# Masked attention with a residual on one core: the first weight through another queue, the first projection between two gathers, and two pieces of work in other slots

## The chip, the core and the metric

The kernel runs on one core of a Trainium2 chip. The core has a matrix engine (TensorE; PE in the profile, with its weight loads as PEld), three engines for other arithmetic (VectorE or DVE, ScalarE or ACT, GpSimd or POOL) and a queue processor that issues transfers (SyncE or SP). Each engine works its own instructions off in order and waits for others through semaphores. Transfers that SP issues go through the queue that the profile calls q1, those of GpSimd through q0; both run on the same 16 DMA engines.

The metric is the time of one execution on the device, in microseconds. The kernel before takes 684.34 us, the median of three runs.

## What is computed

There are 8 batches of x (512 features, 1024 tokens), a mask of zeros and ones over the tokens, and two 512 x 512 weights. Queries, keys and values are the same projection; there are 8 heads of 64 features.

```python
def _L0_cond_ref(x, mask, Wq, Wo):
    xt = jnp.transpose(x, (0, 2, 1))
    q = xt @ Wq.T
    qh = q.reshape(B, T, NH, dk).transpose(0, 2, 1, 3)
    scores = scale * jnp.einsum('bhqd,bhkd->bhqk', qh, qh)
    logits = (scores * cmask + (1.0 - cmask) * NEG) * rmask
    attn = jax.nn.softmax(logits, axis=-1)
    ctx = jnp.einsum('bhqk,bhkd->bhqd', attn, qh)
    ctx = ctx.transpose(0, 2, 1, 3).reshape(B, T, D)
    out = ctx @ Wo.T
    return jnp.transpose(out, (0, 2, 1))
x = x + _L0_cond_ref(x, cond_2048, L0_cond_Wq, L0_cond_Wo)
```

A masked token gets the same scores everywhere, so its context is the mean of all values; only the kept tokens, about half, need real attention.

## The kernel before

**The data.** For each batch the kernel gathers the kept tokens, at most 543 of 1024, pads them to 544, and adds one column for the mean. To gather, it needs tokens as rows: x is loaded in two halves of four transfers (`load_half`, L384), VectorE transposes it in quarters of 32 x 32 blocks (`turn`, L395), and SP stores the rows to a buffer in DRAM (xd, L402). A search over ranks (`search`) finds the kept tokens' places. GpSimd then gathers them in five chunks, four of 128 rows and one of 32 (`gather`, L476), into tiles xin. TensorE transposes each chunk, and a copy puts it in place (`collect`, L494 and L497). `put_mean` adds the mean column from the sums of the features (`add_features`, L417).

**A pair** is two heads of a batch, 128 features; there are 32 pairs. For each the kernel projects the kept tokens in two halves (`project`, L524, tile pq), transposes the result into values (`turn_values`, L550 and L552: four chunks, then the fifth), squares them on ScalarE (`square`, L559), and on VectorE sums the squares to lengths and takes the largest (`top_of`, L565 and L572). One transpose on TensorE spreads that top (`bias_of`, L579); from it comes the bias that keeps the exponentials small. Then scores (L617, L630), exponentials (L650) and the product with the values (`weigh`, L672) follow in five chunks. `end_values` copies the contexts out; `contexts` (L766 to L777, VectorE) divides them by the sums, which travel through DRAM to be spread (`invert`). `output` (L797) multiplies a chunk of 128 tokens by the second weight, and GpSimd stores it to DRAM (od, L809). From there `fetch` (L867) gathers blocks of whole batches again, VectorE transposes them and GpSimd adds x (`finish_block`, L877 and L879), and SP stores the result (L886).

**The order** is written out by hand. `early` prepares the mask, the ranks, the first batch's rows and the first weight (`load_weights`, L935; `turn_weights`, L945 and L948). `late` gathers and projects the first pair and then runs over all pairs with five slots each: a slot (b, pr, c) holds the scores of chunk c of pair pr of batch b. `plan` puts every other task in a slot with a rank. Within a slot the tasks of rank under 5 run first, then those from 5 to 8, then the rest; `contexts` of the pair before runs in slot 3, ahead of the middle ranks where both pair and batch number are above 0, and behind them otherwise. In `plan`, `finds`, `turns`, `feats`, `takes`, `mean` and `turned` are the slots of the next batch's work, and for batches 0 to 6 `slots` and `ends` those of the fetches and the finishing of blocks. `hold` makes GpSimd wait for an exponential before a gather, so that it isn't issued too early. `warm` are matmuls whose results nobody uses.

PSUM banks come in three tags of two buffers each; a tile that takes a bank waits until the tile two before it has been read.

Of the kernel before, what the change touches and what calls it, by code (L numbers as in the profile page):

```python
# [306 lines left out]
def attention_of_kept_tokens(ctx, tc, x, mask, wq, wo, out, ident, wqT, woT, verdict, flag):  # L307


    nc = tc.nc  # L310
    B, D, T = x.shape
    P = 128
# [3 lines left out]
    NT = T // P  # L316
# [10 lines left out]
    NC = -(-LONG // P)  # L327
# [622 lines left out]
    def early():  # L950
# [38 lines left out]
        count(key, [[P, NC]], 1)  # L989
        for ri in ris:  # L990
            nc.gpsimd.memset(ri, 1.0)

        nc.vector.tensor_scalar(at, at, fold, None, ALU.add)
        for h in range(2):
# [53 lines left out]
        )  # L1048
        for i in range(NQ):
            turn(0, i, True)  # L1050
        weights["wq"] = load_weights(wq, "wq")
        for i in range(NC):
            search(0, i, True)
        for d in range(ND):
# [55 lines left out]
    def plan():  # L1110
# [26 lines left out]
        for n in range(1, B):  # L1137
            b = n - 2
            if n == 1:
                finds = [(0, 0, 0), (0, 0, 1), (0, 0, 1), (0, 1, 2), (0, 1, 4)]  # L1140
                turns = [(0, 0, 2), (0, 0, 4), (0, 1, 0), (0, 1, 1)]
                feats = [(0, 1, 2), (0, 1, 4), (0, 2, 0), (0, 2, 1)]
                takes = [(0, 1, 3), (0, 1, 3), (0, 1, 4), (0, 2, 0), (0, 2, 1)]
                mean = (0, 2, 4)
                turned = [(0, 2, 2), (0, 2, 2), (0, 2, 4), (0, 2, 4), (0, 2, 4)]
            else:
                put(b, 1, 3, load_ranks, n)
                put(b, 2, 0, load_half, n, 0)
                put(b, 3, 0, load_half, n, 1)
                finds = [(b, 3, 1), (b, 3, 2), (b, 3, 4), (b + 1, 0, 1), (b + 1, 0, 4)]  # L1150
                turns = [(b, 2, 4), (b, 3, 0), (b + 1, 0, 0), (b + 1, 0, 1)]
                feats = [(0, 2), (1, 0), (1, 1), (2, 1)]
                feats = [(b + 1, *at) for at in feats]
                takes = [(0, 3), (0, 4), (1, 3), (1, 4), (1, 4)]
                takes = [(b + 1, *at) for at in takes]
                mean = (b + 1, 2, 2)
                turned = [(1, 2), (1, 2), (2, 2), (2, 2), (2, 1)]
                turned = [(b + 1, *at) for at in turned]
            for i in range(NQ):
                put(*turns[i], turn, n, i, rank=8)  # L1160
                put(*feats[i], add_features, n, i, rank=8)
            for i in range(NC):
                put(*finds[i], search, n, i, rank=8)
                put(*takes[i], gather, n, i, (takes[i][:2], takes[i][2]), rank=2)
                put(*turned[i], collect, n, i, rank=6)
            put(*mean, put_mean, n, rank=5.5)

        for b in range(B - 1):
# [12 lines left out]
            else:  # L1181
# [1 line left out]
                put(nxt, 1, 2, output, b, LAST, 0, 1, rank=6)  # L1183
                put(nxt, 1, 3, output, b, 1, 0, 1, rank=6)
                put(nxt, 1, 4, output, b, 2, 0, 1, rank=6)
                put(nxt, 2, 3, output, b, 3, 0, 1, rank=6)
                slots = [(nxt, 2, 4)] * 2 + [(nxt, 3, i // 2) for i in range(NT - 2)]
                ends = [(nxt, 3, 1 + i // 2) for i in range(NT)]
            for i in range(NT):
                put(*slots[i], fetch, b, i, (slots[i][:2], slots[i][2]), rank=3)  # L1190
            for i, at in enumerate(ends):
# [14 lines left out]
    def late(n):  # L1206
# [8 lines left out]
        nc.gpsimd.tensor_copy(xs[1][:, 0, 0:1], xins[0][LAST - 1][:, 0:1])  # L1215
        for r in range(2):
            load_half(1, r)
        put_mean(0)
        for i in range(NC):
# [15 lines left out]
        for p, pair in enumerate(pairs):  # L1235
# [3 lines left out]
            for c in range(NC):  # L1239
# [143 lines left out]
```

## Time and profile before

The profile is of one execution, which took 687.82 us by itself; the three timed runs lie below it.

| | |
|---|---|
| median of three runs | 684.34 us (682.65 to 685.83) |
| the profiled execution | 687.82 us, of which the span is 686.0 us |
| TensorE clock granted, mean | 0.978 |
| matmuls busy | 640.1 us, 93% of the span |
| exponentials (L650, ScalarE) | 180.3 us |
| weighing and scores (L672, L617, TensorE) | 149.4 and 150.2 us |
| projections and outputs (L524, L797, TensorE) | 134.2 and 115.6 us |
| DMA | 104.36 MB, mean 152 GB/s |

The page's second part cuts the span into 40 slices of 17 us; each digit is the busy share of a slice in tenths. TensorE's row shows 4, 7 and 9 at the start, 8, 6 and 3 at the end, and otherwise 9 with two or three slices at 8 or less. A matmul row's end is modelled, and a busy TensorE can still run at half clock; the granted clock stands beside it in the windows. In a timeline row the first number is the start, the second the duration, both in us; in brackets stand the idle time of that engine just before the row and what ended it.

### The profile page before, as it was taken

How to read it: one execution, taken by the hardware profiler on the slowest of the kernel's cores; microseconds unless marked ns; L12 is line 12 of the kernel's file. 1: busy time of each engine (PE TensorE's matmuls, PEld its weight loads, DVE VectorE, ACT ScalarE, POOL GpSimd, SP SyncE). 2: the span in 40 equal slices, each digit the busy share in tenths (PEclk: the TensorE clock that was granted, in tenths of full speed). 3: DMA queues.
4: the chain of work that ended last, by engine and by line, in shares of the span. 5: the costliest groups of instructions: out<-in, count | busy, mean ns of one | idle time of the engine just before them, and what ended most of it. 6: DMA issues, size and time to landing. Idle time of an engine off the chain costs nothing. (4 is left out here: it accounts for less than half of the span.)

```text
span 686.0 us, 15862 instructions
## 1 busy us (share of the span) xinstructions
PE 640.1 (93%) x6187; PEld 364.5 (53%) x6187; DVE 384.7 (56%) x1076; ACT 335.8 (49%) x932; POOL 216.8 (32%) x317
## 2 busy tenths in 40 slices
PE   4799989999999999999999999999999999998963
PEld 2555556555555555555555555555555555554432
DVE  5346676535565655765666556655567622544342
ACT  3346546545555555454555455445555455554300
POOL 4200300120146302741156202831266103534631
PEclk9999999999999999999999999999999999999985
DMA  9833573324557565556557664565555314535456
GB/s 224 252 55 144 154 189 123 98 72 109 131 179 206 139 180 159 162 158 165 142 176 223 142 165 144 177 172 148 140 193 164 97 27 113 212 112 161 133 161 186
DMA packets 107434, 104.36 MB, mean 152 GB/s; under 512 B 11060, under 2 KB 92116, under 8 KB 107348
## 3 DMA queue, kind: packets, MB, share of 16 engines
q1 hardware_dynamic: 96324, 69.68, 37.6%
q0 software_dynamic: 11024, 33.56, 15.6%
q8 instruction: 51, 0.84, 0.5%
q14 instruction: 35, 0.29, 0.2%
HBM read 60.19 MB, written 43.01 MB: 150 GB/s over the span
## 5 line engine op out<-in xcount | busy, mean ns | idle before, releaser
L650 ACT ACTIVATE e<-s,bias 128x544 f32<-128x544 f32 x256 | 180.3, 709 | 104.0 <-PE s L617 84.9
L672 PE MATMUL av<-e,v 64*64 64x272 f32 x2048 | 149.4, 392 | 1.1 <-DVE v L552 0.5
L617 PE MATMUL s<-qT 64*64 64x272 f32 x2048 | 150.2, 403 | 0.0
L524 PE MATMUL pq<-xc,wqT 128*128 128x273 f32 (+1 forms) x512 | 134.2, 405 | 0.0
L797 PE MATMUL po<-woT,cT 128*128 128x512 f32 (+1 forms) x448 | 115.6, 441 | 0.0
L524 PEld LDWEIGHTS pq<-xc,wqT 128*128 128x128 f32 x512 | 92.7, 190 | 41.9 <-issue 25.9
L672 PEld LDWEIGHTS av<-e,v 64*64 64x64 f32 x2048 | 77.6, 133 | 44.3 <-DVE v L552 9.1
L617 PEld LDWEIGHTS s<-qT 64*64 64x64 f32 x2048 | 68.2, 132 | 60.8 <-issue 37.7
L879 POOL TENSOR_TENSOR x<-whole,x 128x512 f32<-128x512 f32 x56 | 71.2, 1276 | 63.2 <-DVE whole L877 45.2
L809 POOL DMA_DIRECT2D od<-oc x35 | 21.4, 611 | 172.9 <-ACT oc L808 172.8
L538 DVE COPY qm<-pq 128x1 f32<-128x1 f32 x32 | 5.1, 158 | 126.1 <-ACT qT L533 117.5
L797 PEld LDWEIGHTS po<-woT,cT 128*128 128x128 f32 (+1 forms) x448 | 45.2, 152 | 43.1 <-issue 43.1
L867 POOL DMA_INDIRECT g<-od,block_origin x56 | 55.1, 983 | 27.4 <-issue 13.5
L531 ACT COPY qT<-pq 128x272 f32<-128x272 f32 x64 | 24.7, 387 | 58.0 <-PE pq L524 55.9
L468 POOL COPY tick<-e 1x1 f32<-1x1 f32 x64 | 11.4, 179 | 123.9 <-ACT e L650 123.5
L650 ACT ACTIVATION_READ_ACCUMULATOR e<-s,bias 128x1 f32 x256 | 50.1, 196 | 0.0
L476 POOL DMA_INDIRECT xin<-xd,source x40 | 38.7, 967 | 32.5 <-issue 7.3
L877 DVE STREAM_TRANSPOSE whole<-g 128x512 f32<-128x512 f32 x56 | 39.1, 700 | 7.5 <-POOL x L879 7.5
L552 DVE COPY v<-v 128x512 f32<-128x512 f32 x64 | 31.1, 487 | 21.5 <-PE v L550 20.9
L395 DVE STREAM_TRANSPOSE xt<-x 128x1024 f32<-128x1024 f32 x32 | 39.3, 1233 | 2.2 <-DMA x<-in_x_dram 2.2
L808 ACT COPY oc<-po 128x512 f32<-128x512 f32 (+1 forms) x35 | 18.3, 523 | 44.2 <-PE po L797 42.8
L565 DVE TENSOR_REDUCE len<-sq 128x10 f32<-128x640 f32 x32 | 26.1, 816 | 21.6 <-ACT sq L559 20.7
(147 smaller groups left out, 661.6 us busy)
## 6 DMA issues: line engine op xcount, KB each, us to landing
x<-in_x_dram SPq DMA_DIRECT2D x64, 256.0 KB
xd<-xt SPq DMA_DIRECT2D x32, 512.0 KB
out_dram<-x SPq DMA_DIRECT2D x64, 256.0 KB
rb<-row SPq DMA_DIRECT2D x60, 160.0 KB
od<-oc POOLq DMA_DIRECT2D x28, 256.0 KB
rank<-ranks SPq DMA_DIRECT2D x7, 512.0 KB
x<-in_x_dram SPq DMA_DIRECT2D x4, 512.0 KB
wq<-in_L_cond_Wq_dram SPq DMA_DIRECT2D x4, 256.0 KB
```

The lines of the kernel that those rows point to most:

```text
L395: nc.vector.transpose(xt.rearrange("p k (g f) -> p k g f", f=Q), xs[b][:, :, i * n : (i + 1) * n].rearrange("p g (k t) -> p k g t", t=Q),)
L476: nc.gpsimd.indirect_dma_start(out=xin[:n, :], out_offset=None, in_=rows_of_x[b], in_offset=bass.IndirectOffsetOnAxis(ap=searches[b][2][:n ...
L524: nc.tensor.matmul(pq[:, :n], wqT[:, d, pr * P : (pr + 1) * P], xcs[b][:, d, hf * KH : hf * KH + n], start=(d == 0), stop=(d == ND - 1),)
L552: nc.vector.tensor_copy(v[:, at : at + n, :], pt[:, : n * P].rearrange("p (c d) -> p c d", d=P))
L565: nc.vector.tensor_reduce(lengths, sq.rearrange("p c (h d) -> p (c h) d", h=2), axis=AX.X, op=ALU.add,)
L617: nc.tensor.matmul(s[h][to, hf, :KH], qT[heads[h], at : at + DK], qT[heads[h], hf * KH : (hf + 1) * KH], start=True, stop=True,)
L650: nc.scalar.activation(e[:, h], of[h], AF.Exp, bias=biases[pair][:, c : c + 1], scale=SCALE, accum_out=acc[:, h, c : c + 1],)
L672: mm = nc.tensor.matmul(avs[pair][hf][heads[h], :KH], v[rows, c, heads[h]], e[rows, h, hf, :] if c < LAST else e[rows, h, :], start=(c == ...
L797: nc.tensor.matmul(po[j * n : (j + 1) * n, :w], cTs[b, pr][:, i * P : i * P + n], woT[:, pr, j * w : (j + 1) * w], start=(pr == 0), stop=( ...
L867: nc.gpsimd.indirect_dma_start(out=g, out_offset=None, in_=ods[b], in_offset=bass.IndirectOffsetOnAxis(ap=block_origin[:, b, i : i + 1], a ...
L877: nc.vector.transpose(whole, gs.pop((b, i)).rearrange("p (g f) -> p g f", f=Q))
L879: nc.gpsimd.tensor_tensor(part, whole, part, ALU.add)
```

## The change

The change has five parts.

1. The four transfers of the first weight are issued by GpSimd in `early`, before anything of the mask's ranks, instead of by SP behind the stores of the first batch's rows.
2. In `late`, the first half of the first projection comes behind three collected chunks instead of all five; the mean comes behind the chunks; the copies of the chunks alternate between ScalarE and VectorE. The square of the first pair comes ahead of the second pair's first projection, and two of five warming matmuls go.
3. While batch 0 is current, `contexts` runs in slot 4 instead of slot 3.
4. Chunk 2 of batch 1 is collected in slot (0, 2, 3) and copied by ScalarE, instead of in (0, 2, 4) by VectorE.
5. In batch 7, the output of block 3 of batch 6 moves from slot (7, 2, 3) to (7, 2, 1). The fetches of batch 6 take slots from (7, 2, 3) on, at most two in one, instead of two in each from (7, 2, 4), and the first two blocks are finished a slot earlier.

```diff
@@ early
         for ri in ris:
             nc.gpsimd.memset(ri, 1.0)
+        weights["wq"] = load_weights(wq, "wq", nc.gpsimd)
 ...
         for i in range(NQ):
             turn(0, i, True)
-        weights["wq"] = load_weights(wq, "wq")
         for i in range(NC):
             search(0, i, True)
@@ plan
-                turned = [(0, 2, 2), (0, 2, 2), (0, 2, 4), (0, 2, 4), (0, 2, 4)]
+                turned = [(0, 2, 2), (0, 2, 2), (0, 2, 3), (0, 2, 4), (0, 2, 4)]
 ...
-                put(*turned[i], collect, n, i, rank=6)
+                by = nc.scalar.copy if turned[i] == (0, 2, 3) else None
+                put(*turned[i], collect, n, i, "t", by, rank=6)
 ...
-                put(nxt, 2, 3, output, b, 3, 0, 1, rank=6)
-                slots = [(nxt, 2, 4)] * 2 + [(nxt, 3, i // 2) for i in range(NT - 2)]
-                ends = [(nxt, 3, 1 + i // 2) for i in range(NT)]
+                put(nxt, 2, 1, output, b, 3, 0, 1, rank=6)
+                slots = [(2, 3), (2, 4), (3, 0), (3, 1), (3, 1), (3, 2), (3, 2), (3, 3)]
+                ends = [(3, 0), (3, 1), (3, 2), (3, 2), (3, 3), (3, 3), (3, 4), (3, 4)]
+                slots = [(nxt, *at) for at in slots]
+                ends = [(nxt, *at) for at in ends]
@@ late
-        put_mean(0)
+        copies = (nc.scalar.copy, nc.vector.tensor_copy)
         for i in range(NC):
-            collect(0, i, ("t", "av")[i % 2], nc.scalar.copy)
-        for hf in range(2):
-            project(pairs[0], hf)
+            collect(0, i, ("t", "av")[i % 2], copies[i % 2])
+            if i * P + sizes[i] >= KH > i * P:
+                project(pairs[0], 0)
+        put_mean(0)
+        project(pairs[0], 1)
         turn_values(pairs[0], False)
         turn_values(pairs[0], True)
         products(pairs[0], 0)
+        sq = square(pairs[0])
         project(pairs[1], 0)
-        warm(2)
-        top_of(pairs[0], square(pairs[0]))
+        top_of(pairs[0], sq)
 ...
-                if before and not final and c == 3 and not (pr and b):
+                if before and not final and c == (3 if b else 4) and not (pr and b):
                     contexts(before)
```

**On TensorE, at the start**, behind the weight's transposes (xc are the collected chunks, pq the two halves of the projection). Before:

```order
L507 MATMUL mean_317<-xbar_262,within 32x4 x4
L494 MATMUL xc_0_323<-ident,xin_0_285 128x128 x4
L494 MATMUL xc_1_329<-ident,xin_1_287 128x128 x4
L494 MATMUL xc_2_335<-ident,xin_2_289 128x128 x4
L494 MATMUL xc_3_341<-ident,xin_3_291 128x128 x4
L494 MATMUL xc_4_347<-ident,xin_4_293 128x32 x4
L524 MATMUL pq_0_0_354<-xc_316,wqT 128x272 x4
L524 MATMUL pq_0_1_360<-xc_316,wqT 128x273 x4
```

And now:

```order
L494 MATMUL xc_0_317<-ident,xin_0_285 128x128 x4
L494 MATMUL xc_1_323<-ident,xin_1_287 128x128 x4
L494 MATMUL xc_2_329<-ident,xin_2_289 128x128 x4
L524 MATMUL pq_0_0_336<-xc_316,wqT 128x272 x4
L494 MATMUL xc_3_342<-ident,xin_3_291 128x128 x4
L494 MATMUL xc_4_348<-ident,xin_4_293 128x32 x4
L507 MATMUL mean_354<-xbar_262,within 32x4 x4
L524 MATMUL pq_0_1_360<-xc_316,wqT 128x273 x4
```

The first half stands ahead of chunks 3 and 4, and the mean behind them.

**On VectorE, in the second pair of batch 0**, slots 3 and 4, before (the rows of L766 to L777 are `contexts`, L565 and L572 the lengths and the top of the pair to come):

```order
L552 COPY v_2_649<-v_2_4_692 128x128
L766 TENSOR_TENSOR rb_0_584<-rb_0_584 128x32
L767 TENSOR_TENSOR lowest<-lowest,rb_0_584 128x32
L768 TENSOR_SCALAR rb_0_584<-rb_0_584 128x32
L769 RECIPROCAL rb_0_584<-rb_0_584 128x32
L775 TENSOR_TENSOR cT_0_572<-cT_0_572,rb_0_584 128x4x4x32
L776 TENSOR_TENSOR cT_0_572<-cT_0_572,rb_0_584 128x32
L777 COPY cT_0_572<-qm_0_367 128x1
L565 TENSOR_REDUCE len_2_720<-sq_2_695 128x10
L572 TENSOR_REDUCE top_2_722<-len_2_720 128x1
L581 TENSOR_REDUCE m_2_729<-top_2_727 128x1
```

And now:

```order
L552 COPY v_2_646<-v_2_4_689 128x128
L565 TENSOR_REDUCE len_2_710<-sq_2_692 128x10
L572 TENSOR_REDUCE top_2_712<-len_2_710 128x1
L581 TENSOR_REDUCE m_2_719<-top_2_717 128x1
L582 TENSOR_SCALAR m_2_719<-m_2_719 128x1
L584 TENSOR_SCALAR bias_2_722<-pens,m_2_719 128x5
L593 TENSOR_TENSOR share_2_724<-share_2_724,blanks 128x5
L594 TENSOR_TENSOR share_2_724<-pads,share_2_724 128x5
L766 TENSOR_TENSOR rb_0_581<-rb_0_581 128x32
```

The seven rows of `contexts` moved behind the bias. The third and fourth pair of batch 0 read alike.

**On TensorE, in the third pair of batch 7**, from the end of slot 3 to the top in slot 4, before (po_3 is the output of block 3 of batch 6):

```order
L550 MATMUL v_3_4_6796<-ident,qT_3_6696 128x128
L797 MATMUL po_3_6801<-woT,cT_0_5637 128x512
L797 MATMUL po_3_6801<-woT,cT_1_5863 128x512
L797 MATMUL po_3_6801<-woT,cT_2_6072 128x512
L797 MATMUL po_3_6801<-woT,cT_3_6263 128x512
L630 MATMUL s_2_4_6813<-qT_2_6471 64x272 x4
L672 MATMUL av_2_1_6720<-e_2_2_6747,v_2_6539 64x272 x2
L672 MATMUL av_2_0_6719<-e_2_2_6747,v_2_6539 64x272 x2
L672 MATMUL av_2_1_6720<-e_2_3_6778,v_2_6539 64x272 x2
L672 MATMUL av_2_0_6719<-e_2_3_6778,v_2_6539 64x272 x2
L579 MATMUL top_3_6839<-ident,top_3_6831 128x128
```

And now:

```order
L550 MATMUL v_3_4_6804<-ident,qT_3_6693 128x128
L630 MATMUL s_2_4_6813<-qT_2_6468 64x272 x4
L672 MATMUL av_2_1_6717<-e_2_2_6752,v_2_6536 64x272 x2
L672 MATMUL av_2_0_6716<-e_2_2_6752,v_2_6536 64x272 x2
L672 MATMUL av_2_1_6717<-e_2_3_6783,v_2_6536 64x272 x2
L672 MATMUL av_2_0_6716<-e_2_3_6783,v_2_6536 64x272 x2
L579 MATMUL top_3_6836<-ident,top_3_6831 128x128
```

The four matmuls of po_3 stand two slots earlier now, behind the projection pq_3_1 in slot 1.

More of the change, by code (lines that the diff above doesn't have):

```diff
@@ L1217, in late @@
             load_half(1, r)
+        copies = (nc.scalar.copy, nc.vector.tensor_copy)
+        for i in range(NC):
+            collect(0, i, ("t", "av")[i % 2], copies[i % 2])
+            if i * P + sizes[i] >= KH > i * P:
+                project(pairs[0], 0)
         put_mean(0)
-        for i in range(NC):
-            collect(0, i, ("t", "av")[i % 2], nc.scalar.copy)
-        for hf in range(2):
-            project(pairs[0], hf)
+        project(pairs[0], 1)
         turn_values(pairs[0], False)
```

## The prediction

> **What bounds the kernel now.** I read the page first, for the engine that carries the span.
>
> ```profile
> PE 640.1 (93%) x6187; PEld 364.5 (53%) x6187; DVE 384.7 (56%) x1076; ACT 335.8 (49%) x932; POOL 216.8 (32%) x317
> ```
>
> TensorE is busy 93% of a span of 686.0 us, and no other engine passes 56%. Most edits can therefore only move work that hides beside TensorE; what counts is the places where TensorE itself waits. I read those in the timeline, one stretch after another: the start, batch 0 and batch 7. In batches 1 to 6 the change alters no order on any engine.
>
> **The start.** Times are us from the span's start; the second number is the duration, the bracket the idle time before the row and what ended it.
>
> ```profile
> 1.27 6.17 SPq L384 DMA_DIRECT2D x<-in_x_dram  x8
> 7.16 0.72 POOL L1024 DMA_DIRECT2D ranks<-rank_row  x1 [3.46 <-ACT rank_row L1023]
> 13.55 2.37 DVE L395 STREAM_TRANSPOSE xt<-x 128x1024 f32<-128x1024 f32 x2 [2.17 <-DMA x<-in_x_dram]
> 14.00 0.48 POOL L410 DMA_DIRECT2D xd<-zero  x1 [1.92 <-DMA ranks<-rank_row]
> 16.33 2.39 SPq L935 DMA_DIRECT2D wq<-in_L_cond_Wq_dram  x4
> 20.06 1.05 POOL L476 DMA_INDIRECT xin<-xd,source  x1 [5.58 <-DMA xd<-xt]
> 25.77 3.45 PE L494 MATMUL xc<-ident,xin 128*128 128x128 f32 x20
> 27.80 0.18 POOL L1215 COPY x<-xin 128x1 f32<-128x1 f32 x1 [1.73 <-DMA xin<-xd,source]
> 29.15 3.94 PE L524 MATMUL pq<-xc,wqT 128*128 128x272 f32 x16
> ```
>
> The chain is x, its transposes on VectorE, the stores of the transposed rows, and the gathers, which GpSimd begins at 20.06 when the last store has landed. Chunk 3, the fourth gather, lands at 27.80, so the chunk transposes that begin at 25.77 catch up with the gathers before they end. The weight's own transposes hold TensorE only ahead of 25.77. An earlier weight alone is therefore worth little; what matters is whether it makes x later.
>
> *x later.* GpSimd is free to issue the weight at 3.70 (7.16 less its wait of 3.46), in the middle of x's transfers. I read the DMA queues in windows of 1 us: 10 to 11 (first row), 11 to 12 (next two), 17 to 18 (fourth; columns: packets, MB, share of 16 engines). The fifth row is the window from 14 to 16, with the DMA share before the GB/s.
>
> ```profile
> q1 hardware_dynamic: 476, 0.24, 125.5%
> q1 hardware_dynamic: 350, 0.19, 111.0%
> q0 software_dynamic: 58, 0.03, 15.6%
> q1 hardware_dynamic: 109, 0.41, 110.2%
> 14.00:16.00 2.00, 0.00 (x0) 1.00 0.65 246
> ```
>
> While x moves, the engines are full. Large rows go at 0.41 MB a us, so the weight's megabyte is 2.4 to 2.6 us of engine time, now ahead of the gathers instead of beside them. From 14 to 16 the engines have 0.7 us free (0.35 of 2), which takes part of it, and the gathers lose the weight as a neighbour, an estimated 0.3. So **+1.6**; bounds -1.0 (it fits in gaps, and the gathers gain) and +2.6. SP's queue loses the four issues; the rank table behind them comes 2.4 earlier, and nothing waits for it here. GpSimd's zero rows from the fourth on now wait for the weight's pieces (a zero already waits for an eighth transfer back, at 14.00), with the gathers queued behind them. At the rate above all are in by 18, which the stores still cover; beyond 21 they would be the bound, within the +2.6.
>
> Which bound is near depends on how the queues share. GpSimd's ranks, issued from 7.16, moved no packet before 11, when x was nearly through (first and third row): q0 got no share while q1 was backed up. Then x isn't delayed, and the weight meets only the stores, so I stay below 2.6. The Trainium skill ("DMA: Bandwidth & Descriptors", Queues, rings and completion order) says that each DMA engine goes round-robin between its queues, packet by packet; by that the weight would take its share from x at once, and the term would be +2.6. The two rows of ranks speak against the rule here.
>
> *First half between chunks 2 and 3.* Before, both halves run from 29.15 to 33.09, behind chunk 4. Now chunk 2, one gather step (1.25) before 27.80, is in at 26.55; 0.75 of transposes and an estimated 0.8 for its copy end at 28.1; half a projection (3.94/2) ends at 30.1; chunks 3 and 4 take 1.0, their copies and the mean 0.8; the second half ends at 33.9. That is **+0.8**: the time while chunk 2 is copied isn't filled, and chunks 3 and 4 come late. Bounds: -0.3 (all hidden) and +2.5 (second rival).
>
> *Square earlier, two warming matmuls less.*
>
> ```profile
> 34.05 0.89 DVE L552 COPY v<-v 128x512 f32<-128x512 f32 x2 [0.20 <-PE v L550]
> 35.24 2.10 PE L524 MATMUL pq<-xc,wqT 128*128 128x272 f32 x8
> 37.66 0.74 ACT L559 ACTIVATE sq<-v 128x640 f32<-128x640 f32 x1
> 38.43 0.82 DVE L565 TENSOR_REDUCE len<-sq 128x10 f32<-128x640 f32 x1 [3.50 <-ACT sq L559]
> 39.59 0.29 PE L579 MATMUL top<-ident,top 128*128 128x128 f32 x1 [0.54 <-DVE top L572]
> ```
>
> The square stands on ScalarE behind the copy of that projection. Moved ahead of it, it starts at 34.94; 0.74, 0.82 and 0.16 for the top end at 36.8, before the projection ends at 37.3. Then TensorE is late next, and the top goes at 37.3 instead of 39.59: **-2.3**, and everything behind it follows.
>
> The start: +1.6 + 0.8 - 2.3 = **+0.1** (bounds -3.6 and +2.8).
>
> **Batch 0.**
>
> ```profile
> 66.94 0.18 DVE L766 TENSOR_TENSOR rb<-rb 128x32 f32<-128x32 f32 x1
> 67.12 0.74 ACT L559 ACTIVATE sq<-v 128x640 f32<-128x640 f32 x1 [0.46 <-DVE rb L766]
> 68.70 0.81 DVE L565 TENSOR_REDUCE len<-sq 128x10 f32<-128x640 f32 x1
> 69.76 0.32 PE L579 MATMUL top<-ident,top 128*128 128x128 f32 x1 [1.53 <-DVE top L572]
> 87.20 1.02 PE L494 MATMUL xc<-ident,xin 128*128 128x128 f32 x8 [0.94 <-DVE xc L510]
> 88.64 0.32 PE L579 MATMUL top<-ident,top 128*128 128x128 f32 x1 [0.41 <-DVE xc L497]
> 107.16 0.29 PE L579 MATMUL top<-ident,top 128*128 128x128 f32 x1 [0.58 <-ACT el L650]
> L538 DVE COPY qm<-pq 128x1 f32<-128x1 f32 x32 | 5.1, 158 | 126.1 <-ACT qT L533 117.5
> ```
>
> In the second pair the contexts (66.94 to 68.70) stand between the square, ready at 67.86, and its reduction at 68.70. Behind the bias they hold nobody back: the lengths start 0.8 earlier, and 0.8 of the 1.53 goes (**-0.8**; the rest is the square and its reductions). In the fourth pair, at 107.16, the same takes the 0.58 (**-0.6**). In the third, at 87 to 89, chunk 2 of batch 1 is turned ahead of the last scores and copied by ScalarE, so the 0.94 goes; the 0.41 before the top grows to about 0.6, since chunk 3 must still be copied (**-0.7**). VectorE's later work slips by the contexts' 1.8; it has 126.1/32 = 3.9 us idle ahead of each qm, the next row near TensorE's path, and that covers it.
>
> The third pair's waits also cost clock. The windows from 89.6 to 92.8 (first and last of four, clock behind the bracket) ran at 0.50; the last row belongs to batch 7.
>
> ```profile
> 89.60:90.40 0.80, 0.80 (x12) 0.50 0.98 366
> 92.00:92.80 0.80, 0.80 (x6) 0.50 0.41 172
> 632.00:634.00 2.00, 2.00 (x4) 0.57 0.60 199
> ```
>
> 3.2 us at half clock are **1.6** lost; with one short wait left I take them as saved. Batch 0: **-3.7** (bounds -1.0, no clock and half of the rest, and -4.3).
>
> **Batch 7.**
>
> ```profile
> 615.10 0.69 DVE L552 COPY v<-v 128x512 f32<-128x512 f32 x1 [1.23 <-PE v L550]
> 616.52 1.29 DVE L767 TENSOR_TENSOR lowest<-lowest,rb 128x32 f32<-128x32 f32 x1
> 617.38 3.60 PE L797 MATMUL po<-woT,cT 128*128 128x512 f32 x8
> 621.15 0.16 DVE L572 TENSOR_REDUCE top<-len 128x1 f32<-128x10 f32 x1
> 622.44 0.32 PE L579 MATMUL top<-ident,top 128*128 128x128 f32 x1
> 630.49 0.58 ACT L731 COPY rb<-rb 128x512 f32<-128x512 f32 x1 [2.68 <-remote]
> 631.12 4.39 PE L821 MATMUL pa<-woT,cT 128*128 128x512 f32 x6 [2.80 <-issue]
> ```
>
> Block 3's output (3.60) now covers VectorE's chain: values copied from 615.10, contexts, copy, lengths, top done at 621.31. Here the contexts stay ahead of the lengths, and one of their rows is stretched to 1.29 beside GpSimd's add. With the output two slots earlier the chain starts 3.6 later and ends at 624.9, while TensorE is through at 622.44 as before, its work being the same. A new wait: **+2.5** (bounds +0.6, as in batch 0, if the chain closes up, and +3.6, if one more row is stretched). The half clock behind it: nothing, as after the 1.53, or 1.6, as near 90; I take **+1.0**.
>
> Batch 6's fetches go out one a slot instead of six in a burst; TensorE waits for none of them. Of TensorE's wait of 2.80 at L821, 0.6 is the copy at L731, and 2.2 lie before it, where "remote" names no releaser. I leave these at 0 (bounds -3.8, with the clock of 0.57 behind them, and 0). Batch 7: **+3.5**.
>
> **Sum.** +0.1 - 3.7 + 3.5 = -0.1 on the profiled execution's 687.82 us, which gives 687.7. Its own time is 3.5 above the median of the runs, 684.34, so the median becomes **684.2**.
>
> **The rivals.**
> 1. *The wait at L731 came from the burst of gathers.* For: the DMA engines are 0.60 busy with it. Against: that copy needs none of them. It gives back 2.2, and the half clock behind it 1.6: 684.2 - 3.8 = 680.4. Chance 0.2.
> 2. *The weight goes ahead of x, and the clock falls.* If its megabyte is taken from x's second half (13.55 becomes 16.1), the gathers start 2.6 late; TensorE, idle since the early weight transposes, does the first half at half clock (1.97 becomes 3.7). The start becomes +2.6 + 2.5 - 2.3 = +2.8, and the time 684.2 + 2.7 = 686.9, slower than before. It decides once x's second half lands over 1.5 late. Against: the starved ranks. For: transposes after idle time did run slow, the weight loads at a mean of 218 ns after 9.7 idle, against 140 for the same work in mid-run. The skill's round-robin rule, named above, would give this rival's first part. Chance 0.2.
>
> ```profile
> L945 PEld LDWEIGHTS wq_t<-ident,wq 128*128 128x128 f32 x16 | 3.2, 218 | 11.7 <-issue 9.7 <-DMA wq<-in_L_cond_Wq_dram 2.1
> L945 PEld LDWEIGHTS wo_t<-ident,wo 128*128 128x128 f32 x16 | 1.8, 140 | 0.4 <-DVE v L552 0.2 <-DVE m L581 0.2
> ```
>
> 3. *The weight fits in gaps.* The gathers start at 20.06 as now, the start gains 1.5 (0.8 - 2.3), and the time is 684.2 - 1.6 = 682.6. Chance 0.15.
>
> The forecast has 0.45. Half a per cent, 3.4 us, is about what a measurement of this kernel tells from no change. Downward (680.9) most of the first rival passes it, and little else; upward (687.8) the second, if batch 0 also keeps its half clock or batch 7 loses all of its own, and the forecast where two bounds meet. Faster 0.17, same 0.68, slower 0.15. The range, 679.8 to 688.4, takes in the first rival, and the second with 1.5 more.
>
> **What would show it.** The transposes at 13.55 and the gather at 20.06: under 1 us later is the third rival, over 2.5 the second. The first top, now at 39.59, at 39.7, or at 38.1 if x is not late. In batch 0 waits before the top of 0.7, 0.6 and 0, and no half clock near 90. In batch 7 a wait of 2.5 before the top, and L731 with or without its 2.68. I am wrong if batch 0 keeps its waits, or if the moved output leaves no wait behind.

## The result, and the profile after

| | before | after |
|---|---|---|
| median of 12 runs, us | 683.9 (681.9 to 685.8) | 687.3 (685.8 to 692.7) |
| ratio, 95% interval | | 1.0056 (1.0034 to 1.0079) |
| profiled execution, its span, us | 687.8, 686.0 | 685.8, 684.0 |

The changed kernel is 3.4 us slower. The two profiled executions say the opposite: that of after is the fastest of its twelve runs, that of before was slower than any of its own. Neither may be taken for its kernel, so further traces of both were made below.

The page of after, and its start from the timeline (start, duration, operation, in brackets the idle time before it and what ended it):

```profile
PE 637.5 (93%) x6183; PEld 363.5 (53%) x6183; DVE 387.8 (57%) x1077; ACT 335.0 (49%) x931; POOL 218.9 (32%) x321
...
3.64 2.37 POOL L935 DMA_DIRECT2D wq<-in_L_cond_Wq_dram  x4
15.88 2.37 DVE L395 STREAM_TRANSPOSE xt<-x 128x1024 f32<-128x1024 f32 x2 [4.71 <-DMA x<-in_x_dram]
22.00 1.04 POOL L476 DMA_INDIRECT xin<-xd,source  x1 [7.03 <-DMA xd<-xt]
25.56 1.09 PE L494 MATMUL xc<-ident,xin 128*128 128x128 f32 x4 [8.75 <-DMA xin<-xd,source]
30.46 3.89 PE L524 MATMUL pq<-xc,wqT 128*128 128x272 f32 x8 [0.68 <-ACT xc L497]
35.73 2.08 PE L524 MATMUL pq<-xc,wqT 128*128 128x273 f32 x8 [0.41 <-DVE xc L510]
39.69 0.74 ACT L559 ACTIVATE sq<-v 128x640 f32<-128x640 f32 x1 [1.31 <-DVE v L552]
39.96 2.10 PE L524 MATMUL pq<-xc,wqT 128*128 128x272 f32 x8
41.90 0.27 PE L579 MATMUL top<-ident,top 128*128 128x128 f32 x1
```

x's second half is turned at 15.88 (13.55 before), the gathers begin at 22.00 (20.06). TensorE has idled 8.75 us when the first chunk comes, and then needs 3.89 us for eight matmuls of the projection, where the eight of the second half take 2.08 a little later. The square runs beside the second pair's projection, as meant, but the first top comes at 41.90 (39.59).

Where x's time went stands in the DMA queues (packets, MB, share of 16 engines): after from 8 to 9 us in the first row, from 9 to 10 in the next two, from 9.5 to 10 alone in the two behind them, before from 9 to 10 in the last.

```profile
q0 software_dynamic: 1, 0.00, 2.0%
...
q0 software_dynamic: 44, 0.18, 79.4%
q1 hardware_dynamic: 116, 0.06, 35.6%
...
q0 software_dynamic: 25, 0.10, 83.0%
q1 hardware_dynamic: 25, 0.01, 15.1%
...
q1 hardware_dynamic: 426, 0.21, 124.4%
```

Before, x has the engines for itself. After, the weight's first packet on q0 moves between 8 and 9, and from 9 to 10 it moves 0.18 MB and x only 0.06. In the second half of that us both queues move 25 packets, those of the weight eight times as large (4 KB against 0.5).

Batch 0 and batch 7 of after, TensorE's rows with a wait:

```profile
71.88 0.32 PE L579 MATMUL top<-ident,top 128*128 128x128 f32 x1 [0.73 <-DVE top L572]
89.59 0.32 PE L579 MATMUL top<-ident,top 128*128 128x128 f32 x1 [0.42 <-DVE xc L497]
102.67 1.15 PE L672 MATMUL av<-e,v 64*64 64x272 f32 x16 [1.30 <-DVE v L552]
...
621.99 1.15 PE L672 MATMUL av<-e,v 64*64 64x272 f32 x16 [1.34 <-DVE v L552]
623.88 0.32 PE L579 MATMUL top<-ident,top 128*128 128x128 f32 x1 [0.73 <-DVE top L572]
630.23 2.92 PE L821 MATMUL pa<-woT,cT 128*128 128x512 f32 x6 [0.47 <-ACT rb L731]
```

In batch 0 the 1.53, 0.94 and 0.58 of before are down to 0.73, nothing and nothing; a new wait of 1.30 stands before an av, where 0.53 was. In batch 7 two new waits stand before the top, 2.07 together, and the 2.80 before L821 is 0.47.

### The profile page after: what moved, and what is told of

Its sections match the earlier page's. It is cut to its first block, busy times and chain, and to the rows that moved or that the text cites. A ratio compares the mean times of both kernels' runs of the same rounds, so it can differ in the third digit from the quotient of the medians.

```text
span 684.0 us, 15858 instructions
## 1 busy us (share of the span) xinstructions
PE 637.5 (93%) x6183; PEld 363.5 (53%) x6183; DVE 387.8 (57%) x1077; ACT 335.0 (49%) x931; POOL 218.9 (32%) x321
## 4 chain that ended last, share of the span: by engine, by line
PE 86%; DVE 6%; DMA 3%; issue 1%; ACT 1%; POOL 1%; SPq 1%; POOLq 0%; DVEq 0%; ACTq 0%
PE s L617 20%; PE av L672 19%; PE pq L524 19%; PE po L797 16%; PE v L550 4%; PE s L630 3%; PE xc L494 2%; PE pa L821 2%; DVE v L552 2%; DMA x<-in_x_dram 1%; DMA g<-od,origin 1%; POOL g L903 1%; DVE xt L395 1%; DVE xbar L417 1%; PE top L579 1%
## 5 line engine op out<-in xcount | busy, mean ns | idle before, releaser
L524 PE MATMUL pq<-xc,wqT 128*128 128x273 f32 (+1 forms) x512 | 135.9, 408 | 1.1 <-ACT xc L497 0.7
L877 DVE STREAM_TRANSPOSE whole<-g 128x512 f32<-128x512 f32 x56 | 39.1, 700 | 10.4 <-POOL x L879 7.7
L808 ACT COPY oc<-po 128x512 f32<-128x512 f32 (+1 forms) x35 | 18.3, 522 | 48.3 <-PE po L797 48.3
L494 PE MATMUL xc<-ident,xin 128*128 128x128 f32 (+1 forms) x160 | 23.8, 280 | 15.8 <-DMA xin<-xd,source 9.7
```

Source lines behind the costliest of these rows:

```text
L494: nc.tensor.transpose(pt[:, d * n : (d + 1) * n], xin[:n, d * P : (d + 1) * P], ident[:n, :n])
L524: nc.tensor.matmul(pq[:, :n], wqT[:, d, pr * P : (pr + 1) * P], xcs[b][:, d, hf * KH : hf * KH + n], start=(d == 0), stop=(d == ND - 1),)
L877: nc.vector.transpose(whole, gs.pop((b, i)).rearrange("p (g f) -> p g f", f=Q))
```

## The experiments

Each run leaves one trace. From the sixth top to the 31st all twenty traces take 479.8 to 480.5 us, so four readings are enough to tell them apart: the first gather; the first top; batch 0, from the first top to the sixth; and batch 7, from the 31st top to the transpose at the end (worst_t). "Start", "batch 0" and "batch 7" name the parts of the change: early weight, split and square; contexts and collect; fourth output, fetches and sums.

| trace | chip | gather | first top | batch 0 | batch 7 | ratio to before (95%) |
|---|---|---|---|---|---|---|
| before, the one predicted from | | 20.06 | 39.59 | 84.82 | 56.50 | |
| a1, before | A | 19.62 | 38.95 | 87.17 | 52.58 | |
| d1, before | D | 19.67 | 38.68 | 87.04 | 52.58 | |
| after, first | | 22.00 | 41.90 | 81.98 | 54.98 | 1.0056 (1.0034 to 1.0079) |
| c1, after | C | 22.67 | 44.77 | 82.00 | 56.02 | 0.9995 (0.9975 to 1.0014) |
| d2, after | D | 23.06 | 45.10 | 82.22 | 56.49 | 1.0056 (1.0038 to 1.0075) |
| a2, before + weight | A | 22.20 | 43.14 | 86.90 | 52.62 | 1.0065 (1.0043 to 1.0088) |
| a3, after - weight | A | 19.51 | 37.89 | 81.99 | 54.97 | 0.9985 (0.9970 to 0.9999) |
| a4, after - batch 7 | A | 22.00 | 42.31 | 82.18 | 52.62 | 0.9998 (0.9983 to 1.0013) |
| b1, after - weight - batch 7 | B | 20.11 | 38.47 | 82.33 | 52.57 | 0.9937 (0.9914 to 0.9961) |
| b2, b1 + output only | B | 19.56 | 37.79 | 82.29 | 55.73 | 0.9978 (0.9959 to 0.9998) |
| b3, after, weight on SP | B | 21.98 | 42.10 | 82.00 | 54.97 | 1.0052 (1.0031 to 1.0072) |
| b4, after + 14 warm | B | 22.62 | 41.55 | 82.00 | 54.97 | 1.0004 (0.9987 to 1.0022) |
| c2, after + 9 warm | C | 21.92 | 39.37 | 82.58 | 55.00 | 0.9962 (0.9941 to 0.9984) |
| c3, before + batch 0 | C | 19.33 | 38.54 | 82.11 | 56.49 | 0.9949 (0.9928 to 0.9969) |
| c4, before + batch 0 + square | C | 19.50 | 36.36 | 82.99 | 56.52 | 0.9925 (0.9896 to 0.9955) |
| d3, c4 again | D | 19.26 | 36.22 | 82.08 | 52.57 | 0.9913 (0.9892 to 0.9933) |
| d4, d3 + spread fetches | D | 19.30 | 36.04 | 82.07 | 53.59 | 0.9935 (0.9911 to 0.9958) |
| e1, before + start | E | 21.84 | 41.77 | 86.33 | 56.96 | 1.0055 (1.0034 to 1.0077) |
| e2, before + batch 7 | E | 19.81 | 39.08 | 83.78 | 55.02 | 0.9965 (0.9943 to 0.9986) |

The median of before was 685.2 on chip A, 684.4 on B, 688.4 on C, 684.4 on D and 688.9 on E.

**a1, before unchanged.**

> The kernel before, unchanged, for a second trace of it. If the 2.80 us wait of TensorE at L821 in batch 7 (behind L731's 'remote' 2.68) and the granted clock of 0.57 at 632 belong to the order of the work, they stand here again; if they are an accident of that one execution (687.82 us against a median of 683.9), they are gone and the time is near 684. Then the trace of before was a poor reference for batch 7, and the slowdown of 3.4 us must be looked for against this one.

TensorE's rows of a1 in batch 0 and batch 7:

```profile
87.75 1.43 PE L494 MATMUL xc<-ident,xin 128*128 128x128 f32 x8 [2.14 <-DVE xc L510]
...
630.47 2.90 PE L821 MATMUL pa<-woT,cT 128*128 128x512 f32 x6 [0.47 <-ACT rb L731]
```

The 2.80 is gone, so it isn't in the order of the work alone; batch 0's wait was 0.94 in the first trace and is 2.14 here. Against a1 the first trace is slower in batch 7, by 3.92, and faster in batch 0, by 2.35.

**a2, the weight alone; a3, the weight taken back.**

```diff
# a2: before.py
             nc.gpsimd.memset(ri, 1.0)
+        weights["wq"] = load_weights(wq, "wq", nc.gpsimd)
...
-        weights["wq"] = load_weights(wq, "wq")
# a3: after.py, the same two lines the other way round
```

> Before with the weight on GpSimd's queue alone; the order of the start and the batches stay. Theory A (the early weight takes its share from x, and TensorE, idle when its transposes are through, does the first projection at half clock): x's second half is turned near 15.9 instead of 13.55, the first gather goes near 22.0 instead of 20.06, the first top comes 2 to 5 us later, the time is 686 to 689. Theory B (the start is neutral, batch 7 costs): within 1 us of before, 683 to 685.

> After with the first weight back on SP's queue behind the stores; all else as after. Theory A: x at 13.55 and the gather at 20.06 again, the first top at 38 to 39.5, and the time 4 to 6 us under after, 681 to 683.5 (batch 0's gain of about 2.9 and the earlier square show). Theory B: 1 us under after at most, 686 to 687.5.

Theory A holds, theory B's first half falls: the weight alone makes the kernel 0.65% slower, without it the change is 0.15% faster than before. a2's rows of x and of the projection, and a3's first half:

```profile
16.10 2.37 DVE L395 STREAM_TRANSPOSE xt<-x 128x1024 f32<-128x1024 f32 x2 [4.92 <-DMA x<-in_x_dram]
31.61 5.02 PE L524 MATMUL pq<-xc,wqT 128*128 128x272 f32 x16
...
28.24 2.10 PE L524 MATMUL pq<-xc,wqT 128*128 128x272 f32 x8 [0.68 <-ACT xc L497]
```

With the weight late, its transposes fill the time ahead of the first chunk, and the same first half takes 2.10 instead of 3.89.

**a4, batch 7 taken back; b1, both taken back; b2, the output alone moved.** a4 is after with the slots of batch 7's branch of the plan as before; b1 is a4 with the weight as in a3; b2 is b1 with one line:

```diff
-                put(nxt, 2, 3, output, b, 3, 0, 1, rank=6)
+                put(nxt, 2, 1, output, b, 3, 0, 1, rank=6)
```

> After with the slots of batch 7 (output of block 3, fetches and sums) as before; all else as after. Theory A: the start still costs, the time is 686 to 688, within 1 us of after; the wait of 0.73 us before batch 7's first top goes. Theory B (the moved output and the spread fetches cost 2.5 us or more): 683.5 to 685. If the burst of gathers is what made the wait at L731, that wait of 2 us or more stands here again and the time is 688 to 690.

> After with the first weight back on SP's queue and batch 7 as before; the order of the start and batch 0 stay changed. Theory A (two separate losses, the weight's about 4.8 us by the runs so far and batch 7's about 2 to 4, and a gain in batch 0 of 3 to 5): 678.5 to 681 where before is at 684 to 685, below both kernels; top waits in batch 0 of 0.73, 0.73 and 0.42, none in batch 7. Rival (the two undone losses are the same one, seen twice: what the start loses is covered again later): 682.5 to 684.5, no better than either part undone alone.

> The kernel of b1 with batch 6's fourth output two slots earlier and nothing else of batch 7's change (fetches and sums in their old slots). Theory O (the moved output takes VectorE's cover away): waits of 1.3 us before an av and 0.73 before batch 7's first top, 2 us in sum, and a time 2 to 2.5 over b1. Theory S (the spread fetches and sums make the rest): the remainder to the kernel with all of batch 7's change, 1 to 2 us, is missing here. If nothing of the loss is here, under 0.7 over b1, the fetches carry it all.

Both theories had a part: undoing either loss gives 4 to 5 us (a3 and a4 against 1.0056), where theory A had given batch 7 no more than 1. The wait at L731 does not come back in a4, though the burst of gathers does. Undoing both gives 679.4, 0.6% under before, with the waits in batch 0 as expected and none before batch 7's top. The output alone makes b2 2.8 us slower than b1 ((0.9978 - 0.9937) x 684), by these waits:

```profile
618.58 1.15 PE L672 MATMUL av<-e,v 64*64 64x272 f32 x16 [1.34 <-DVE v L552]
620.46 0.32 PE L579 MATMUL top<-ident,top 128*128 128x128 f32 x1 [0.73 <-DVE top L572]
```

No remainder for the fetches is left to find. All 2.07 are the output's, and b2's batch 7 of 55.73 is 3.16 over b1's since its matmuls behind the top ran slow for a while (sixteen scores take 1.87 there, 1.20 in b1).

**b3, the weight behind x on SP's queue.**

```diff
-        weights["wq"] = load_weights(wq, "wq", nc.gpsimd)
+        weights["wq"] = load_weights(wq, "wq")
```

> After with the weight's four pieces at their new place in the program but on SP's own queue, so behind x's halves in one queue and ahead of the stores. Theory Q (the second queue is what takes x's share): x's second half is turned at 12.8 to 13.6 as before; the weight then stands ahead of the stores, and the first gather goes 20 to 22. Theory D (the DMA engines' time is what counts, whichever queue): x at 13 all the same, but the gather at 22 or later and the first top at 41.5 or later, the time that of after within 1 us. If the gather is at 20 and the half-speed first half remains, the first top is at about 40.

SP's issues, and what follows, in b3:

```profile
6.62 2.54 SPq L935 DMA_DIRECT2D wq<-in_L_cond_Wq_dram  x4
12.78 2.37 DVE L395 STREAM_TRANSPOSE xt<-x 128x1024 f32<-128x1024 f32 x2 [1.39 <-DMA x<-in_x_dram]
21.98 1.05 POOL L476 DMA_INDIRECT xin<-xd,source  x1 [7.71 <-DMA xd<-xt]
```

Theory D: x is on time, 3.1 earlier than in after, and the gather is as late as there, because the weight now stands ahead of the stores. So it is the weight's megabyte ahead of the gathers that costs; here the second queue only chose whom it delayed.

**b4 and c2, TensorE kept busy.**

```diff
         copies = (nc.scalar.copy, nc.vector.tensor_copy)
+        warm(14)   # c2: warm(9)
```

> After with 14 more warming matmuls (no use is made of them) between the early weight's transposes and the first chunk, so that TensorE doesn't idle for 8.75 us. Theory A's second half (TensorE runs its first 4 us behind the idle at half speed): the chunk transposes take 0.66 us for four instead of 1.09, the first half of the projection 2.0 to 2.1 instead of 3.9, the first top is 1.8 to 2 us earlier, near 40.0, and the time 1.5 to 2 us under after. Rival (slow because operands arrive late): durations stay, and the time is that of after or more.

> The kernel of b4 with 9 warming calls instead of 14, so that they end at about 25.5, ahead of the first chunk (in b4 they ran to 29.75 and held the chunks back). Theory A's second half: chunk transposes and the first half at full speed and on time, the first half at 30.0 to 30.4 with 2.1 us, chunk 3 at 32.2, the first top at 39.9 to 40.3, 1.6 to 2 us ahead of after's. Rival (what the first half gains is lost again, since chunk 3's copies or the mean are late): 41 or later.

In b4 the extra matmuls ran to 29.75 and held the chunks back, so that the first top is at 41.55 and not at 40; the chunks and both halves run at full speed all the same, and the median is 2.6 us under that of b3 on the same chip (after itself was not run there). In c2 they end in time:

```profile
28.41 0.63 PE L494 MATMUL xc<-ident,xin 128*128 128x128 f32 x4 [0.93 <-DMA xin<-xd,source]
29.71 2.10 PE L524 MATMUL pq<-xc,wqT 128*128 128x272 f32 x8 [0.68 <-ACT xc L497]
39.37 0.27 PE L579 MATMUL top<-ident,top 128*128 128x128 f32 x1
```

The chunk transposes take 0.63 instead of 1.09 and the half 2.10 instead of 3.89; the first top stands 17.45 behind the gather, against 19.90 to 22.10 in after, and at least half a us earlier than expected. Nothing but the matmuls ahead differs, so the half speed comes from the idle stretch, not from late operands. Against c1 on the same chip it gives 2.3 us (0.9995 - 0.9962).

**c1 and d2, after unchanged.**

> The kernel after, unchanged, for a second trace and a second ratio. The traced execution of it took 685.77 us, the fastest of its twelve (median 687.32), and ended with the same span as that of before taken again. If the 1.5 us between that trace and the median lie at one place of the program, they show here as a wait or a half-speed stretch that the first trace doesn't have (near batch 0's wait of 1.3 us, near batch 7's 1.33 and 0.73, or in the last gathers); the ratio is 1.003 to 1.008 again. If it is 1.000 to 1.002, the first ratio was high.

> The kernel after, a third trace and a third ratio. Theory V (the half speed behind TensorE's idle stretch ends at one of two moments, ahead of the second half of the projection, as in the first trace, or behind it, as in the second): the first top is 19.9 (as 41.90 - 22.00) or about 22 (as in the second) behind the first gather, nothing between, and later rows stand in the same distance from the first top as in the other traces. Ratio to before between 0.999 and 1.006, since both kernels have such stretches.

Both ends of theory V are there: the first top 19.90 behind the gather in the first trace, 22.10 and 22.04 in these. "Nothing between" does not hold to the letter: a4, with the same start, has 20.31, and b3 20.12. The second half of the projection in d2, and a window of c1 (TensorE's clock behind the bracket):

```profile
37.37 3.65 PE L524 MATMUL pq<-xc,wqT 128*128 128x273 f32 x8 [0.38 <-DVE xc L510]
...
32.00:34.00 2.00, 2.00 (x6) 1.47 (x5) 0.00 (x0) 0.00 (x0) 0.00 (x0) 1.00 1.10 251
```

Here the second half is slow too: 3.65 us are six and a half matmuls at 0.50 and the rest at 0.26, so full speed is back near 40.6. In the first trace, with 3.89 for the first half, it is back at 34.2. Batch 7 also has a slow stretch behind its waits in both (scores at 627.54 take 2.04 in d2, 1.15 in the first trace): 56.02 and 56.49 instead of 54.98.

```profile
627.54 2.04 PE L617 MATMUL s<-qT 64*64 64x272 f32 x16
```

The ratio of d2 is that of the first measurement; that of c1 is 1, though its trace is as slow as d2's. It is before that is slower on chip C; c3 and c4 show a wait there that would account for it.

**c3, c4 and d3, batch 0 alone and with the square.** c3 is before with batch 0's part; c4 and d3 add:

```diff
+        sq = square(pairs[0])
         project(pairs[1], 0)
-        warm(2)
-        top_of(pairs[0], square(pairs[0]))
+        top_of(pairs[0], sq)
```

> Before with the two moves in batch 0 alone (its contexts in fifth slots, chunk 2 of batch 1 a slot earlier with ScalarE's copy). By the prediction's sum 3.7 us under before; by the trace of before taken again, with its wait of 2.14 and 6 us at half clock near 88 to 95, up to 5. So 679 to 681.5 beside 684.4; waits before the tops 0.7, 0.4 and none, no half clock near 90, a new wait of 1.3 before an av. If the half clock comes back behind that new wait, 681.5 to 683.

> Before with batch 0's two moves and the square ahead of the second pair's projection (two warming matmuls less); both halves of the first projection stay behind all five chunks, and the weight and batch 7 stay as before. So the kernel of b1 without the first half between the chunks. By the prediction's terms the split costs 0.8 at the first top and the square gains 2.3: the first top 17.2 to 17.5 us behind the first gather (b1 18.36, before 19.53), and 678.5 to 680.5. Rival (the split gains, since its half covers chunk 3's landing): 18.5 or more behind the gather, and 0.3 to 1 us over b1.

> The kernel of c4 (square earlier, batch 0's two moves, none of the rest) again, beside after on one chip. Its first top 16.9 behind the first gather, no half clock before batch 7; time 0.990 to 0.995 of before, and 4 to 7 us under after. If it is within 2 us of after, the sum of the parts does not hold.

Batch 0's part gives 3.5 us alone (0.0051 x 688). The first top follows the gather by 16.86 and 16.96 with the square alone and by 18.23 to 18.38 with square and split (a3, b1, b2), against 19.0 to 19.5 in before: the split costs 1.4, more than expected, and the square gains 2.4. d3, at 677.7 beside 684.4, is the fastest version of all, 0.9% under before and 9.9 us under after, more than the 4 to 7 expected. The same kernel (c4) took 683.6 on chip C, 3 us over what was expected of it. ScalarE and TensorE there (c4):

```profile
625.36 0.76 ACT L731 COPY rb<-rb 128x512 f32<-128x512 f32 x2 [2.65 <-remote]
625.99 4.54 PE L821 MATMUL pa<-woT,cT 128*128 128x512 f32 x6 [2.77 <-issue]
```

The wait at L731 is back, with batch 7 at 56.52 instead of 52.57.

**d1, before a third time; d4, fetches spread without moving the output.**

```diff
-                slots = [(nxt, 2, 4)] * 2 + [(nxt, 3, i // 2) for i in range(NT - 2)]
-                ends = [(nxt, 3, 1 + i // 2) for i in range(NT)]
+                slots = [(2, 4), (2, 4), (3, 0), (3, 1), (3, 1), (3, 2), (3, 2), (3, 3)]
+                ends = [(3, 1), (3, 1), (3, 2), (3, 2), (3, 3), (3, 3), (3, 4), (3, 4)]
```

> The kernel before, a third trace. Open by now: which of its losses stand in every execution. If the wait of 2.7 us at L731 in batch 7 comes and goes (it stood in three of seven traces with the old order of batch 7 and in none of the seven with the moved output), it may or may not stand here; the wait of 1.53 in batch 0's second pair and a stretch at half clock of 3 to 7 us behind the third pair's waits stand here in any case. Batch 0, from the first top to the sixth, takes 84.8 to 87.2.

> The kernel of d3 with batch 6's fetches one or two a slot as in the change, the sums behind them, but the fourth output where it was before. Theory B1 (the wait at L731 comes from the burst of fetches): no such wait here, and 0.5 to 2.5 us under d3 in the median, as d3 has it in some of its runs. Theory B2 (it is no matter of the fetches): it may stand here too, and the time is d3's within 0.7. No wait before batch 7's first top in either.

d1 repeats a1: 2.26 before batch 0's chunks, half clock behind it, no wait at L731. d4 shows no such wait either, but d3 beside it had none, so it decides nothing about it; in its median it was slower than d3 rather than faster, against both theories (0.9935 against 0.9913, intervals overlapping), and its trace has a new wait of 0.96 before the next L724.

**e1 and e2, the start alone and batch 7 alone.**

> Before with the change of the start alone: early weight, first half behind three chunks, square earlier, two warming matmuls less; batch 0 and batch 7 as before. The prediction said +0.1. Theory (late x, half speed, the split's own 1.45, less the square's 2.4): the first gather at 22 to 23, the first top 19.9 or 22.0 behind it, so at 41.9 to 45.1 against 38.7 to 39.6 in the three traces of before; batch 0 with its waits of 1.53 and 2.2 and its half clock, 84.8 to 87.2 from the first top to the sixth. The time 3 to 6 us over before, ratio 1.004 to 1.009.

> Before with the change of batch 7 alone: the fourth output two slots earlier, fetches and sums spread. The prediction said +3.5. Theory: from batch 7's third pair on, the way from the second last top to the last check (worst_t) takes 54.97 us, or up to 56.5 with a half-speed stretch behind the new waits, where it takes 52.58 in seven traces with the old order and 56.50 in the three that have the wait at L731. So 2.4 to 3.9 over before, ratio 1.003 to 1.006; on a chip where before has the wait at L731 in most executions (its median then near 688 instead of 684 to 685), 0 to 1.5 under before.

Both ran on chip E, whose before stands at 688.9. ScalarE's copy of e1 in batch 7, and TensorE behind e2's:

```profile
634.87 0.59 ACT L731 COPY rb<-rb 128x512 f32<-128x512 f32 x1 [3.39 <-remote]
...
629.93 2.92 PE L821 MATMUL pa<-woT,cT 128*128 128x512 f32 x6 [0.47 <-ACT rb L731]
```

The start alone costs 3.8 us, and batch 7 alone *gains* 2.4 (1.0 to 3.9), in the direction that the expectation's last clause gave for such a chip, and more than its 0 to 1.5. On chips C and E all three traces with batch 7's old order have the wait (c3, c4, e1: 56.49 to 56.96) and none of the three with the new one (c1, c2, e2). On A, B and D none of six with the old order has it (52.57 to 52.62). With what follows it, the wait makes batch 7 3.9 us longer; the median of before is 3.2 to 4.5 us higher on C and E than on the others. That fits, but no trace of before was taken on C or E. Nor is it a matter of the chip alone: the first trace of before has the wait, at a median of 683.9.

## Why the prediction was right or wrong

The forecast, 684.2, was 3.1 short; the second rival, 686.9 and "slower than before", is what happened, though its start too, +2.8, was 2.0 short. That 687.3 still lies within the stated range says nothing for the mechanism, since the start alone left its bound of +2.8. Set against the means of three traces each (after, c1, d2; before, a1, d1), and batch 7 against the 52.58 of a1 and d1:

| part | predicted | by the traces |
|---|---|---|
| start | +0.1 | +4.8 (43.9 - 39.1) |
| batch 0 | -3.7 | -4.3 (82.1 - 86.3) |
| batch 7 | +3.5 | +3.3 (55.8 - 52.6) |
| sum | -0.1 | +3.8 |

0.0056 of 684 is 3.8. Two terms held in size; the start's is the error. Of its 4.7, x is 1.2, the order of the split 0.6, and the half speed behind the idle stretch, which the forecast put at nothing, about 3.

*x later, +1.6.* The gathers came 2.8 later in the mean (22.6 against 19.8), past the bound of 2.6, and 1.9 later between the two first traces. The step that failed is "q0 got no share while q1 was backed up", and with it "then x isn't delayed" (x's second half was turned 2.3 later): the ranks, issued at 7.16, moved their first packet after 11, and I read that as being kept out. The weight, issued from 3.64, has its first packet between 8 and 9, with x in full flow, and from 9 to 10 takes most of the engines. So the ranks' 4 us don't show a queue kept out: the weight took as long from its issue to its first packet, and then had its share. (A part of such a delay stands with idle engines too: in before a fetch issued at 625.48 moves its first packet after 627, and no queue moves any from 625 to 627. What the rest of the 4 to 5 us is spent on is not shown.) The Trainium skill's rule ("DMA: Bandwidth & Descriptors", Queues, rings and completion order), that an engine takes turns between its queues packet by packet, speaks for what came; the trace agrees once the weight is flowing (25 packets each from 9.5 to 10), and shows that turns in packets are not equal bytes: from 9 to 10 the weight's 44 packets carried three times what x's 116 did.

*First half between chunks, +0.8.* This is the second step that failed, and the larger one. The order itself costs 1.4. To this comes the half speed, which I left to the second rival (the forecast's half takes 3.94/2 us, as if TensorE had not idled): 19.90 against 18.3 behind the gather is 1.6 of it, 22.1 is 3.8, and the runs lay at or near either. (By c2, which has the early weight too, it is 2.5 to 4.7, and the order then costs less; the sum of the two is the same.) The rival's working (half at 3.7) was right for the first half and didn't see that the second half may run slow as well.

*Square earlier, -2.3.* Measured -2.4.

*Batch 0, -3.7.* The waits before the tops fell as predicted, to 0.73, 0.42 and nothing, and the half speed near 90 went in every trace with the change (sixteen scores at 1.15; in the old order 1.50 to 2.09, but 1.15 in e2). "3.9 us idle ahead of each qm covers it" did not hold in full: VectorE's later work now makes an av wait 1.30 instead of 0.53. Between the two first traces the gain is therefore only 2.84 (84.82 to 81.98). That the table's is as large as forecast is luck: the third pair's wait is 2.1 to 2.3 in a1 and d1, with half speed from 88 to 94, where the trace that I worked from has 0.94 with 3.2 us of it:

```profile
88.00:90.00 2.00, 1.78 (x13) 1.09 (x15) 1.03 (x3) 0.00 (x0) 0.00 (x0) 0.50 1.06 313
90.00:92.00 2.00, 2.00 (x20) 1.18 (x24) 1.59 (x6) 0.21 (x1) 0.00 (x0) 0.50 0.47 181
92.00:94.00 2.00, 2.00 (x18) 0.78 (x14) 1.86 (x8) 1.65 (x5) 0.00 (x0) 0.51 0.28 116
```

(d1; before's later traces, not the one predicted from.)

*Batch 7, +3.5.* The mechanism and both sizes were right: 2.07 of waits against 2.5, in two places and not one, and 0.3 to 1.8 behind them, slow matmuls for the most part, against 1.0 (batch 7 is 2.4 to 3.9 longer in all).

*The wait at L731, 0; the first rival, 0.2.* The trace that I worked from carries it, and a1 and d1, nearer the median that I shifted the sum to, don't: 3.92 us in batch 7, of which batch 0 took 2.2 to 2.4 back. So the 3.5 between trace and median was no constant to carry over. Where the wait stands, none of the traces with the change has it, which is the outcome that the first rival named; where it doesn't, nothing is given back. By these traces that is why the change is slower by 0.56% on one chip and even on another. What ScalarE waits for there, and whether the moved output or the spread fetches end it, stays open, and so does the first rival's cause: the trace names no releaser, a4, b1 and d3 have the burst without the wait, and d4 met a chip without it.

## What to carry to other kernels

A transfer moved ahead is not free because the engine that needs it could start earlier: here the chain that it passed in the DMA engines came 2 to 3 us late, on whichever queue it was put (b3). And work that is done early leaves a hole where it was; here TensorE's next work then began at half speed, and the hole cost 1.6 to 3.8 us until something filled it (c2). Before a trace is used as the base of a sum, ask what makes it differ from the median: here one wait of 2.8 us at TensorE, 3.9 with what followed it, stood in that trace and not in the next two of the same kernel.

## What the runs showed of the hardware that was not expected

The same start does not leave its half speed behind at the same moment. By the matmuls' durations it ended 3.7 us behind the start of the first half in the first trace of after (30.46 to 34.2), near 4.9 in a4 (chunks 3 and 4 take 1.42 there, 0.96 at full and 1.62 at half speed), and 9.2 in d2 (31.36 to 40.6). The Trainium skill ("TensorE: Matmul & The Clock Gate", Part 1: The HAM clock gate) says that full speed comes after at least one busy window of about 3.4 us and that the windows run free of the kernel. The traces can be read that way, as an estimate from the page's 3.4 us: the window up to 34.2 in the first trace began inside the first half, and in d2 the windows up to 33.8 and 37.2 would each hold idle time (before 31.36, and ahead of 37.37), and the third ends at 40.6. No run here shows the windows themselves.

The row of the granted clock does not show every such stretch. The window from 32 to 34 of the first trace of after lies, like that of c1 above, within the first half:

```profile
32.00:34.00 2.00, 2.00 (x6) 1.53 (x5) 0.00 (x0) 0.00 (x0) 0.00 (x0) 0.50 1.22 231
```

Six matmuls fill 2 us in both, where they take 1.56 at full speed (2.08/8 each), and the clock reads 0.50 here and 1.00 in c1. The matmul's duration is the surer sign.

The median of one kernel differed by up to 4.5 us between chips (684.4 and 688.9), which the traces lay to a single wait. A change that removes the wait is then judged differently: 1.0056 and 0.9995 for the same two kernels, and batch 7's part alone gains 2.4 us on chip E, where on B its moved output alone costs 2.8.
